# Layer 0 of a four-layer convolution stack: the patch filter and the 3x3 taps as one map of pixels per channel

## The chip, the cores and the metric

The kernel runs on one core of one Trainium2 chip. The metric is device time in microseconds (us). The median of three runs of the kernel before is 7,436.29 us (7,435.15 to 7,444.35).

## The reference, cut to what matters

The input x has the shape (4, 64, 256, 256) in 32-bit floats. Four layers follow one another, each `x = x + layer(groupnorm(x))`, with group normalization over pairs of channels. Only layer 0 is changed:

```python
x = einsum('bchw,oc->bohw', x, w_in)               # 64 -> 384 channels
xp = x in patches of 8 x 8 pixels
x  = irfft2(rfft2(xp) * fft_filter)                # one filter for each channel
x  = conv 3x3, each channel by itself (w_dw), padding 1
x1, x2 = split(x, 2)                               # 192 + 192 channels
x  = gelu(x1) * x2
x  = einsum('bchw,oc->bohw', x, w_out)             # 192 -> 64 channels
```

Both steps between the two einsums are linear in a channel's pixels. The patch filter is a circular convolution inside a patch. The 3x3 taps reach over the edge of a patch by one pixel. Layers 1 to 3 (a 3x3 convolution, a gated one with a threshold, a Fourier layer) are the same in both kernels.

## The kernel before, in words

Layer 0 is written in `_layer0`. An image has 256 rows; a step `t` of the main loop (line 659) takes 8 of them, one row of 32 patches, so that there are 4 x 32 steps and two more to finish. The order of the work on TensorE (PE), VectorE (DVE), ScalarE (ACT) and the queue of SyncE (SP) is written out by hand: inside `with ordered:` instructions run on each of these engines in the order of the program. GpSimd (POOL) is left to the scheduler; it clears borders and issues the stores.

Before the loop, statistics of the first image are gathered (line 312) from 32 loads of 512 KB. The statistics of later images are gathered inside the loop.

A step does the following:

- `normalize_x` (ACT, line 256) normalizes the input; pixels lie side by side on the partitions of two halves of the image.
- `transpose_x` and `transform_x` (PE, lines 396 and 406) turn the patches, so that pixels come to lie on partitions, and take the 64 x 64 patch DFT.
- `expand` (PE, line 419) multiplies by `w_in`, 64 to 384 channels, and DVE multiplies by the filter as it copies the result out of PSUM (line 422).
- `invert` (PE, line 457) takes the inverse DFT, and ACT copies the result into `y` (line 464), which holds 11 rows; the 3 last rows of the step before are copied from its `y` (line 437).
- `depthwise` (PE, line 484) does the nine taps of 256 of the 384 channels, as matmuls with diagonal 32 x 32 weights in sixteen array tiles, accumulated in PSUM. ACT takes the Gelu of the gate channels (line 498) and DVE multiplies by the value channels (line 504).
- `vector_tap` does the nine taps of the other 128 channels: the first on ACT (line 520), eight on DVE (line 522); Gelu and gate follow (lines 530 and 537).
- `project` (PE, lines 550 and 559) multiplies by `w_out`, DVE adds the residual (line 573) and takes the statistics for layer 1's normalization (line 581), and POOL issues the store (line 590).

All PSUM tiles of layer 0 come from `pair`, four tiles of two banks that are taken in turn. The gated result never leaves the core: it goes from `h` and `v` in SBUF into the last matmul.

Of the kernel before, what the change touches and what calls it, by code (L numbers as in the profile page):

```python
# [26 lines left out]
def _patch_dft():  # L27
# [20 lines left out]
    pick = np.array(pick)  # L48
    twice = lambda m: np.concatenate([m, m], 0)
    return twice(fwd.T), twice(inv.T), twice(pick).T  # L50
# [19 lines left out]
def _constants(H, W):  # L70
    f_blk, b_blk, pick = _patch_dft()
# [17 lines left out]
        "c_ident": np.eye(128), "c_avg32": avg32, "c_sel32": sel32, "c_fdft": f_blk, "c_bdft": b_blk, "c_pick": pick, "c_avg": avg, "c_avgp": avgp, "c_avgx": avgx,  # L89
# [5 lines left out]
def _layouts(i):  # L95


    order = np.r_[0:128, HID : HID + 128, 128:HID, HID + 128 : 2 * HID]
# [20 lines left out]
class _Net:  # L119
    def __init__(self, ctx, tc, a):  # L120
# [15 lines left out]
        self.slots = ctx.enter_context(tc.tile_pool(name="slot", bufs=2))  # L136
# [138 lines left out]
    def _layer0(self, ctx, dst):  # L275
# [9 lines left out]
        small = self.small = lambda name: pair(name)[:, 0, :]  # L285
        HW2 = W // 2
        NJ = H // 8
        NS = B * NJ
        Q = 32
        halves = [slice(0, C), slice(C, 128)]  # L290
        quarters = [slice(k * Q, (k + 1) * Q) for k in range(4)]

# [9 lines left out]
        with tc.tile_pool(name="l0a", bufs=1) as p_a:  # L302
            bst0 = new_bst0(0)

            flat = a["x"][0].rearrange("c (s h) w -> (c s) (h w)", s=2)
            avgs = [self.load(name, p_a) for name in ("c_avgp", "c_avgx")]
            for k in range(NJ):
                if k % 2 == 0:
                    two = self.slot(k // 2 % 3, f"st_{k}").rearrange("p r w -> p (r w)")
                t = two[:, 4 * W * (k % 2) : 4 * W * (k % 2 + 1)]  # L310
                nc.sync.dma_start(t, flat[:, 4 * W * k : 4 * W * (k + 1)])
                input_stats(t.rearrange("p (r w) -> p r w", w=W), k, bst0)
            self.group_norm(0, 0, bst0, avgs)

        cp = pool("l0c", 1)
        p_st, p_x, p_r, p_xn = pool("l0st", 2), pool("l0x", 2), pool("l0r", 2), pool("l0xn", 1)
        p_T, p_f, p_u, p_l = pool("l0xT", 1), pool("l0xf", 2), pool("l0up", 2), pool("l0l", 1)
        p_v, p_g, p_h = pool("l0v", 2), pool("l0g", 1), pool("l0h", 2)
        fdft, bdft = self.load("c_fdft", cp), self.load("c_bdft", cp)
        pick, filt = self.load("c_pick", cp), self.load("filt", cp)  # L320
        wdw = self.load("w_dw", cp)
        ps = small("psf")
        nc.tensor.matmul(ps[:, :384], pick, filt, start=True, stop=True)
        flt = cp.tile([128, 1, 384], F32, name="flt")
        nc.vector.tensor_copy(flt[:, 0, :], ps[:, :384])

        win = cp.tile([128, 384], F32, name="win")
        for s in range(2):
            nc.sync.dma_start(win[halves[s]], a["w_in"])

        wout = cp.tile([128, 4, C], F32, name="wout")
        for k in range(4):
            nc.sync.dma_start(wout[quarters[k]], a["w_out"][0:128].rearrange("(g q) o -> q g o", q=Q))
        woutc = cp.tile([128, C], F32, name="woutc")
        for s in range(2):
            nc.sync.dma_start(woutc[halves[s]], a["w_out"][128:HID])

        eye = cp.tile([128, Q], F32, name="eye")
        nc.vector.tensor_copy(eye, self.ident[:, 0:Q])
        for k in range(1, 4):  # L340
            nc.vector.tensor_add(eye, eye, self.ident[:, k * Q : (k + 1) * Q])
# [243 lines left out]
        def store(t, *sides, ins=None):  # L585
            if t not in rt:
                return
# [880 lines left out]
```

## Time and profile before

| what | value |
|---|---|
| median of the runs | 7,436.29 us |
| span of the profiled execution, first to last instruction | 7,394.8 us |
| its own time | taken as its span; the page gives no other |
| median over the span | 41.5 us |
| PE, PEld, DVE, ACT, POOL busy | 97%, 58%, 87%, 53%, 9% |
| mean granted PE clock | 0.971 |
| layer 0 in the span | 0 to 4,851.9 us |
| bytes moved by DMA in the whole span | 873.38 MB, mean 118 GB/s |

The page gives times in us, and means of one instruction in ns. A group's line has the line of the program, the engine, the operation, output<-input, shapes and count; then busy time and the mean of one; then the idle time before it and what ended it. For PE, a shape such as 64*32 is the array tile (rows x columns). A DMA share of 1 is all 16 DMA engines busy.

### The profile page before, as it was taken

Reading aid. Unit: us, or ns where it says so; the run is one execution under the profiler, and the core shown is the slowest. Engines: PE = TensorE matmul, PEld = TensorE weight load, DVE = VectorE, ACT = ScalarE, POOL = GpSimd, SP = SyncE. Lnnn points to the kernel's source line nnn. Section 1 sums busy time; section 2 is a strip of 40 time slices with the busy share of each in tenths; the row PEclk is TensorE's granted clock in tenths of the full one; section 3 lists DMA queues with packets and bytes.
Section 4 is the critical chain, followed back from the end, with each engine's and each line's share of the span. In section 5 each row is a group of like instructions: output and inputs, shape, how many; then the busy total and the mean of one; then the engine's idle time right before and its main releaser. Section 6 shows DMA issues by size and latency. Waiting matters only on the chain. (4 is left out here: it accounts for less than half of the span.)

```text
span 7394.8 us, 396673 instructions
## 1 busy us (share of the span) xinstructions
PE 7148.3 (97%) x188280; PEld 4274.7 (58%) x188280; DVE 6436.5 (87%) x5625; ACT 3928.6 (53%) x4181; POOL 659.3 (9%) x1435
## 2 busy tenths in 40 slices
PE   6999999999999999999999999999999999999998
PEld 4666666666666666666666666633334444444376
DVE  7999999999999999999999999889988888897445
ACT  3444444454454444444445545457778778776211
POOL 0000000000000000000000000011111222222011
PEclk9999999999999999999999999999999999999955
DMA  3222222222222222222111111279986676676989
GB/s 131 64 64 64 61 64 61 61 61 61 61 61 61 61 61 61 61 61 61 47 46 47 47 47 47 60 186 228 230 197 158 169 178 173 172 179 192 354 328 400
DMA packets 650136, 873.38 MB, mean 118 GB/s; under 512 B 43988, under 2 KB 470180, under 8 KB 646468
## 3 DMA queue, kind: packets, MB, share of 16 engines
q1 hardware_dynamic: 567492, 579.51, 29.4%
q0 software_dynamic: 81024, 268.50, 12.5%
q8 instruction: 1477, 24.20, 1.4%
q14 instruction: 143, 1.17, 0.1%
HBM read 579.41 MB, written 268.44 MB: 115 GB/s over the span
## 5 line engine op out<-in xcount | busy, mean ns | idle before, releaser
L484 PE MATMUL psd<-y,diag 32*32 32x512 f32 x73296 | 2535.6, 597 | 12.4 <-issue 10.7
L522 DVE SCALAR_TENSOR_TENSOR v<-y,sb_w_dw,v 128x2048 f32<-128x2048 f32 x1024 | 2391.5, 2335 | 112.1 <-ACT v L520 89.3
L484 PEld LDWEIGHTS psd<-y,diag 32*32 32x32 f32 x73296 | 1526.9, 103 | 858.8 <-issue 338.9
L464 ACT COPY y<-psy 128x512 f32<-128x512 f32 x1536 | 915.6, 660 | 1673.5 <-PE psy L457 1671.7
L422 DVE TENSOR_TENSOR up<-psu,flt 128x768 f32<-128x768 f32 x1024 | 933.1, 952 | 203.9 <-PE psu L419 203.2
L457 PEld LDWEIGHTS psy<-sb_c_bdft,up 64*64 64x64 f32 x49152 | 850.2, 135 | 343.3 <-issue 129.8
L457 PE MATMUL psy<-sb_c_bdft,up 64*64 64x64 f32 x49152 | 919.5, 221 | 25.0 <-issue 22.4
L419 PE MATMUL psu<-win,xf 64*64 64x384 f32 x8192 | 785.0, 488 | 20.9 <-DVE h L504 10.4
L1040 DVE TENSOR_TENSOR q<-xn 128x2313 f32<-128x2313 f32 (+2 forms) x256 | 627.8, 2494 | 1.7 <-ACT xn L256 1.7
L1095 PE MATMUL one<-z,wp 32*32 32x512 f32 x16384 | 594.1, 598 | 17.3 <-issue 13.4
L1041 ACT ACTIVATE q<-q 128x2313 f32<-128x2313 f32 (+2 forms) x256 | 528.9, 2086 | 31.4 <-DVE q L1040 29.9
L498 ACT ACTIVATE h<-psd 128x1024 f32<-128x1024 f32 x258 | 251.2, 1023 | 519.8 <-PE psd L484 519.7
L256 ACT ACTIVATE xn<-x,nb,r 128x1024 f32<-128x1024 f32 (+3 forms) x272 | 486.9, 1793 | 22.2 <-DMA x<-x 8.3
L1095 PEld LDWEIGHTS one<-z,wp 32*32 32x32 f32 x16384 | 368.4, 103 | 225.0 <-issue 82.7
L1054 PE MATMUL div<-q,ones 64*32 64x512 f32 x8192 | 466.2, 594 | 14.3 <-ACT q L1041 9.4
L429 POOL MEMSET y<- 128x22 f32 x384 | 52.2, 136 | 4264.3 <-ACT y L437 3209.8
L419 PEld LDWEIGHTS psu<-win,xf 64*64 64x64 f32 x8192 | 299.5, 134 | 192.1 <-issue 87.7
L1128 POOL DMA_DIRECT2D x<-r x512 | 273.6, 541 | 972.1 <-DVE r L1125 881.2
L854 PE MATMUL m<-t,wk 64*64 64x512 f32 x3072 | 341.1, 588 | 0.0
L1054 PEld LDWEIGHTS div<-q,ones 64*32 64x32 f32 x8192 | 151.8, 107 | 321.1 <-issue 253.6
L537 DVE TENSOR_TENSOR v<-g,v 64x1024 f32<-64x1024 f32 x257 | 313.2, 1219 | 9.3 <-ACT g L530 1.4
L504 DVE TENSOR_TENSOR h<-h,psd 128x1024 f32<-128x1024 f32 x258 | 302.7, 1215 | 7.5 <-PE psd L484 7.0
(156 smaller groups left out, 7400.4 us busy)
## 6 DMA issues: line engine op xcount, KB each, us to landing
x<-x SPq DMA_DIRECT2D x240, 640.0 KB, 6.3
x<-x SPq DMA_DIRECT2D x100, 1024.0 KB, 13.9
x<-in_x_dram SPq DMA_DIRECT2D x256, 256.0 KB, 3.8
x<-o POOLq DMA_DIRECT2D x128, 512.0 KB, 8.1
r<-x SPq DMA_DIRECT2D x512, 128.0 KB, 4.0
x<-r POOLq DMA_DIRECT2D x512, 128.0 KB, 4.0
r<-in_x_dram SPq DMA_DIRECT2D x248, 256.0 KB, 3.8
x<-r POOLq DMA_DIRECT2D x248, 256.0 KB, 3.3
```

The lines of the kernel that those rows point to most:

```text
L256: self.nc.scalar.activation(dst, src, AF.Identity, bias=self.nb[n][p0:p1, b : b + 1], scale=self.r[n][p0:p1, b : b + 1])
L419: nc.tensor.matmul(ps[halves[n], s, 0:384], xf[t][halves[s], n, 4 * g + k], win[halves[s]], start=True, stop=True)
L422: nc.vector.tensor_mul(ups[t, g][:, :, k, :], ps[:, :, 0:384], flt.broadcast_to([128, 2, 384]))
L457: nc.tensor.matmul(ps[halves[c], n, s, :, k, :], up[halves[n], s, k, i * 128 + c * C : i * 128 + (c + 1) * C], bdft[halves[n]], start=True ...
L464: nc.scalar.copy(yt[t][i][:, 3:11, w0 : w0 + 64].rearrange("p r (k n w) -> p n r k w", k=4, n=2), ps[:, :, s])
L484: ins = nc.tensor.matmul(d[q // 2][quarters[j], q % 2], diag[quarters[q], i, k, :], rows_in(t, i, quarters[q], j, dy)[:, :, dx : dx + W], ...
L522: nc.vector.scalar_tensor_tensor(v, s, wdw[:, 2, k : k + 1], v, ALU.mult, ALU.add)
L854: nc.tensor.matmul(rows2(m)[halves[j], s], w[dx][halves[s]], ts[n][halves[s], i, 2 * j : 2 * j + 2, dx : dx + W], start=(dx == 0), stop=(d ...
L1040: nc.vector.tensor_sub(d, p0, p1)
L1041: nc.scalar.activation(d, d, AF.Square)
L1054: ins = nc.tensor.matmul(ps[quarters[j], h], ones[halves[h]], q[n, g, k][halves[h], r + 2 * j : r + 2 * j + 2, o : o + W], start=(m == 0), ...
L1095: ins = nc.tensor.matmul(rows2(ps[g])[quarters[j], k], w[quarters[i]], z[quarters[i], h, 2 * j + dy : 2 * j + dy + 2, dx : dx + W], tile_p ...
```

## The change

Layer 0 is written anew; layers 1 to 3 stay. The patch filter and the taps of a channel become one linear map from the pixels of a patch and its neighbours to output pixels. `tables` works the map's coefficients out on the chip, from `fft_filter`, `w_dw` and a constant. `weights` spreads them into tiles `T` and writes them to a DRAM scratch `wts`, 2 x 64 x 64 x 112 numbers for each of three groups of 128 channels (64 gates and their 64 values). Two tiles `T`, one after the other, share one buffer.

The main loop runs over 20 blocks `p`, five for each image, of 7, 7, 7, 6 and 6 rows of patches. For each group of channels `kb`:

- `expand` makes the 128 channels for up to 8 rows of patches. The patch's 64 normalized pixels are the stationary operand, `w_in` the moving one, so that the result has pixels on partitions with no transpose and no DFT. ACT and DVE copy it out by turns into `u`, one tile with patches as columns (33 for each row of patches, the first of them zero).
- `load_w` brings map tiles from DRAM, one for two calls of `convolve`, through four buffers, requested three tiles ahead.
- `convolve` takes four gates and their four values, in eight array tiles of 64 x 32, with up to 231 patches as columns. One matmul makes the 32 output pixels that need only their own patch; four, accumulated, make the other 32, from the patch, its right, its lower and its diagonal neighbour. ACT takes the Gelu, DVE the gate, and POOL stores the result `h` (four buffers) into a DRAM scratch `g`.

While block `p` is worked on, block `p - 1` is finished in eight units, one for each row of pixels within a patch. `load_g` reads the gated result back with channels on partitions and loads the residual; `project` multiplies by `w_out`, adds the residual, takes the statistics and stores. Units follow the expansion of each group and its maps 5 and 10. SP issues `load_w`, `load_g`, the input and the statistics' loads in the order of the program. The `slots` pool, which layer 0 shared with layer 1, is made after layer 0.

```diff
-    order = np.r_[0:128, HID : HID + 128, 128:HID, HID + 128 : 2 * HID]
+    order = np.concatenate([np.r_[k : k + C, HID + k : HID + k + C] for k in range(0, HID, C)])
...
-        def transform_x(t):
...
-                        nc.tensor.matmul(
-                            ps[halves[s], n, k], x[halves[n], k, halves[s]], fdft[halves[n]], start=True, stop=True
-                        )
...
-        def expand(t, g, k):
...
-                    nc.tensor.matmul(
-                        ps[halves[n], s, 0:384], xf[t][halves[s], n, 4 * g + k], win[halves[s]], start=True, stop=True
-                    )
-            nc.vector.tensor_mul(ups[t, g][:, :, k, :], ps[:, :, 0:384], flt.broadcast_to([128, 2, 384]))
...
-                            nc.tensor.matmul(
-                                ps[halves[c], n, s, :, k, :],
-                                up[halves[n], s, k, i * 128 + c * C : i * 128 + (c + 1) * C],
-                                bdft[halves[n]], start=True, stop=True,
-                            )
...
-                        ins = nc.tensor.matmul(
-                            d[q // 2][quarters[j], q % 2], diag[quarters[q], i, k, :],
-                            rows_in(t, i, quarters[q], j, dy)[:, :, dx : dx + W],
-                            start=(k == 0), stop=(k == 8), tile_position=(q * Q, j * Q),
-                        )
...
-                    nc.vector.scalar_tensor_tensor(v, s, wdw[:, 2, k : k + 1], v, ALU.mult, ALU.add)
...
+        blocks = []
+        for b in range(B):
+            i0, sizes = -1, [7, 7, 7, 6, 6]
+            for n in sizes:
+                blocks.append((b, i0, n))
+                i0 += n
+        NB = len(blocks)
+        u = pool("l0u", 1).tile([128, C, 8 * CW + 2], F32, name="u")
+        p_xn, p_x, p_st = pool("l0xn", 8), pool("l0x", 2), pool("l0st", 2)
+        p_w, p_h = pool("l0w", 4), pool("l0h", 4)
...
+        wts = [dr.tile([2, 64, C, NC], F32, name=f"wt{t}") for t in range(KB)]
...
+        def tables(t):
+            ps = self.small(f"kx_{t}")
+            nc.tensor.matmul(ps[:, 0:289], filt[:, 128 * t : 128 * (t + 1)], kext, start=True, stop=True)
+            nc.vector.tensor_copy(kx.rearrange("p u v -> p (u v)"), ps[:, 0:289])
...
+        def weights(t, copies):
+            for hh in range(2):
+                T = p_a.tile([128, 4, 8, NC], F32, tag="T", name=f"T_{t}_{hh}")
...
+                    copies[k % len(copies)](d, s)
+                for h in range(2):
+                    (nc.sync if t == 0 else nc.gpsimd).dma_start(
+                        wts[t][h, 32 * hh : 32 * hh + 32].rearrange("i c n -> c i n"),
+                        T[halves[h]].rearrange("p a b n -> p (a b) n"),
+                    )
...
+        def expand(p, kb, t, mc):
+            b, i0, n = blocks[p]
+            ps = pair(f"psu_{p}_{kb}_{t}_{mc}")
+            xn = xns[b, i0 + t]
+            for m in range(8):
+                for s in range(2):
+                    for h in range(2):
+                        nc.tensor.matmul(
+                            ps[halves[h], s, m * C : (m + 1) * C],
+                            xn[halves[s], 8 * mc + m].rearrange("p r w -> p (r w)"),
+                            win[halves[s], kb * 128 + h * C : kb * 128 + (h + 1) * C], start=True, stop=True,
+                        )
+            d = u[:, :, t * CW + 1 : (t + 1) * CW].rearrange("p c (s h m) -> p h s c m", s=2, h=2)[:, mc]
+            v = ps.rearrange("p s (m c) -> p s c m", m=8)
+            if mc == 0:
+                nc.scalar.copy(d, v)
+            else:
+                nc.vector.tensor_copy(d, v)
+        def load_w(p, j):
+            if p >= NB:
+                return
+            w = wl[p, j] = p_w.tile([128, 8, NC], F32, tag="w", name=f"w_{p}_{j}")
+            nc.sync.dma_start(
+                w, wts[j // 8][:, :, 8 * (j % 8) : 8 * (j % 8) + 8].rearrange("h i c n -> (h i) c n")
+            )
+        UNITS = ((32, 32, 0), (64, 16, 1), (80, 28, CW), (108, 4, CW + 1))
+        def convolve(p, kb, g):
+            L = CW * blocks[p][2]
+            ps = pair(f"pc_{p}_{kb}_{g}")
+            w = wl[p, 8 * kb + g // 2]
+            tile_of = lambda q, h: dict(tile_position=(h * C, q * Q))
+            for q in range(4):
+                for h in range(2):
+                    nc.tensor.matmul(
+                        ps[quarters[q], h, 0:L], w[halves[h], 4 * (g % 2) + q, 0:32], u[halves[h], 4 * g + q, 0:L],
+                        start=True, stop=True, **tile_of(q, h),
+                    )
+            for k, (c0, m, o) in enumerate(UNITS):
+                for q in range(4):
+                    for h in range(2):
+                        nc.tensor.matmul(
+                            ps[q * Q : q * Q + m, h, L : 2 * L], w[halves[h], 4 * (g % 2) + q, c0 : c0 + m],
+                            u[halves[h], 4 * g + q, o : o + L], start=(k == 0), stop=(k == 3), **tile_of(q, h),
+                        )
+            h = p_h.tile([128, 2 * 7 * CW], F32, tag="h", name=f"h_{p}_{kb}_{g}")[:, 0 : 2 * L]
+            nc.scalar.activation(h, ps[:, 0, 0 : 2 * L], AF.Gelu)
+            nc.vector.tensor_mul(h, h, ps[:, 1, 0 : 2 * L])
+            if p not in gs:
+                gs[p] = p_g.tile([2, HID, Q, L], F32, tag=f"g{L}", name=f"g_{p}")
+            c = kb * C + 4 * g
+            nc.gpsimd.dma_start(
+                gs[p][:, c : c + 4].rearrange("a c p l -> (c p) a l"), h.rearrange("p (a l) -> p a l", a=2)
+            )
...
+        def load_g(p, r):
...
+            g1 = p_1.tile([128, P * 7 * CW], F32, tag="g1", name=f"g1_{p}_{r}")[:, 0 : P * L]
+            g6 = p_6.tile([128, 4 * 7 * CW], F32, tag="g6", name=f"g6_{p}_{r}")[:, 0 : 4 * L]
...
+            for s, p0, q0, m in planes(r):
+                nc.sync.dma_start(g1[:, q0 : q0 + m], gs[p][s, 0:128, p0 : p0 + m])
+                for k in range(2):
+                    lo, hi = max(q0, 4 * k), min(q0 + m, 4 * k + 4)
+                    if lo < hi:
+                        nc.sync.dma_start(
+                            g6[halves[k], lo - 4 * k : hi - 4 * k], gs[p][s, 128:HID, p0 + lo - q0 : p0 + hi - q0]
+                        )
+            rt = rts[p, r] = p_r.tile([128, 7, HW2], F32, tag="r", name=f"r_{p}_{r}")[:, 0 : hi - lo]
+            for s in range(2):
+                nc.sync.dma_start(
+                    rt[halves[s]], xr(a["x"][b], b)[rr][:, j0 : j0 + hi - lo, s * HW2 : (s + 1) * HW2]
+                )
...
+            po = pair(f"po_{p}_{r}")
...
+            for k, q0, q1, d, c0, c1 in groups:
+                for s in range(2):
+                    nc.tensor.matmul(
+                        result(k, q0, q1, c0, c1, s), wo1, moving(g1, q0, q1, d, s),
+                        start=(c0 == 0), stop=False, skip_group_check=True,
+                    )
...
+                    nc.tensor.matmul(
+                        result(k, q0, q1, c0, c1, s), wo6[halves[k]],
+                        moving(g6[halves[k]], q0 - 4 * k, q1 - 4 * k, d, s),
+                        start=False, stop=True, tile_position=(k * C, s * C), skip_group_check=True,
+                    )
...
+                nc.vector.tensor_add(
+                    v, v, po[:, k, c0:c1].rearrange("p (i q j) -> p i q j", i=m, q=q1 - q0)
+                )
...
+            for s in range(2):
+                nc.gpsimd.dma_start(xr(dst[b], b)[rr][:, j0 : j0 + m, s * HW2 : (s + 1) * HW2], rt[halves[s]])
...
+            weights(0, [nc.scalar.copy, nc.vector.tensor_copy, nc.gpsimd.tensor_copy])
...
+            for j in range(3):
+                load_w(0, j)
...
+            for p in range(NB + 1):
+                if p == 1:
+                    ctx_a.close()
+                    p_1, p_6, p_r = pool("l0g1", 2), pool("l0g6", 2), pool("l0r", 3)
+                    load_g(0, 0)
+                    load_g(0, 1)
+                def unit():
+                    r = next(units, None)
+                    if r is None:
+                        return
+                    project(p - 1, r)
+                    k = 8 * (p - 1) + r + 2
+                    if k < 8 * p:
+                        load_g(*divmod(k, 8))
...
+                for kb in range(KB):
+                    for t in range(n + 1):
+                        if 0 <= i0 + t < NP:
+                            for mc in range(2):
+                                expand(p, kb, t, mc)
...
+                    unit()
+                    for g in range(16):
+                        j = 8 * kb + g // 2 + 3
+                        if g % 2 == 0:
+                            load_w(p + j // 24, j % 24)
+                        convolve(p, kb, g)
+                        self.next_norms()
+                        if p == 0 and kb < 2 and g == 0:
+                            tables(kb + 1)
+                            weights(kb + 1, [nc.gpsimd.tensor_copy])
...
+                        if g in (5, 10):
+                            unit()
...
+                for r in units:
+                    project(p - 1, r)
+                if p >= 1:
+                    load_g(p, 0)
+                    load_g(p, 1)
```

## The prediction

> **What bounds the kernel now.** I read the page from the top. The change touches layer 0 alone, so the first question is how much of the span layer 0 is and what limits it.
>
> ```profile
> span 7394.8 us, 396673 instructions
> PE 7148.3 (97%) x188280; PEld 4274.7 (58%) x188280; DVE 6436.5 (87%) x5625; ACT 3928.6 (53%) x4181; POOL 659.3 (9%) x1435
> L484 PE MATMUL psd<-y,diag 32*32 32x512 f32 x73296 | 2535.6, 597 | 12.4 <-issue 10.7
> L522 DVE SCALAR_TENSOR_TENSOR v<-y,sb_w_dw,v 128x2048 f32<-128x2048 f32 x1024 | 2391.5, 2335 | 112.1 <-ACT v L520 89.3
> L457 PE MATMUL psy<-sb_c_bdft,up 64*64 64x64 f32 x49152 | 919.5, 221 | 25.0 <-issue 22.4
> L1054 PE MATMUL div<-q,ones 64*32 64x512 f32 x8192 | 466.2, 594 | 14.3 <-ACT q L1041 9.4
> ```
>
> To see: PE is the bound, and two thirds of its time are layer 0's taps (L484), inverse DFT (L457) and expansion (L419), work that the change replaces. The third line prices a 32x32 tile, the last a 64x32 tile, the shape that the change uses.
>
> Then windows. Layer 0 runs from 0 to 4851.9, where the chain of waits has its first long piece, L854 of layer 1.
>
> ```profile
> 0.00:90.00 90.00, 27.22 (x636) 18.75 (x636) 57.66 (x106) 14.21 (x19) 4.67 (x20) 1.00 0.61 216
> 90.00:4850.00 4760.00, 4688.68 (x150099) 3091.26 (x150096) 4382.56 (x3601) 2330.40 (x2939) 245.66 (x679) 1.00 0.24 58
> 4850.00:5550.00 700.00, 679.39 (x6324) 244.27 (x6324) 614.63 (x588) 499.31 (x403) 80.11 (x144) 0.99 0.88 214
> 7240.00:7300.00 60.00, 51.74 (x256) 41.55 (x250) 30.78 (x50) 7.51 (x13) 9.37 (x13) 0.50 1.04 414
> ```
>
> Columns: stretch, length, busy PE, PEld, DVE, ACT, POOL, clock, DMA share, GB/s. To see: in 90-4850 PE is busy 98.5%, DVE 92%, DMA only 24%. GB/s divided by share is what the DMA engines give when full: 242 in layer 0 (mostly 512-byte runs), 243 in layer 1 (1 KB rows landing at a pitch of 1,032 bytes), 398 at the end (runs of 2 KB and more). No window passes a share of 1.04.
>
> [...] the end window with both queues is full at 1.04. [...] in layer 1 about a fifth of the 1 KB packets took some 46 ns, the rest 64 to 115. [...] L484's psd is evicted in 1.02 us (ACT) and 1.22 us (DVE) per 1,024 elements. [...] the last window shows 0.50 while its DMA is full.
>
> **The change, part by part.** It removes all PE work of layer 0 (4,689 us busy), L522 (2,391), L422 (933) and the copies L437, L464.
>
> PE, added. Maps: 20 blocks x 3 x 16 x 40 = 38,400 matmuls in eight tiles, mean 33 x 6.6 = 218 columns. L1054 gives 466.2/8192 x 8 = 455 ns per eight of 512 columns, 0.89 ns a column: 4,800 x 218 x 0.89 = 930 us. L484's 16 tiles took 553 ns for 512 columns, 98 more; if that is an exposed weight load it adds 4,800 x 98 ns = 470. Expansion: 144 patch rows x 3 x 64 = 27,648 matmuls of 64 columns at L457's 18.7 ns: 517. Last conv: 160 units of some 845 + 422 column times: 180. PE 1,630 to 2,100.
>
> DVE. L504 (1,024 elements, 1,215 ns) and the 512-element L573 (682) give 149 ns + 1.04 per element from PSUM. Gates 960 x 603 ns = 579; half of the evictions, 432 x 1.21 = 525; residual adds 160 x 1.33 = 212 (a stride of 8 elements may double it: the strided L1301 took 600 ns for 256); statistics of the output 189, of the next batch 175. Sum 1,680. ACT: 432 x 1.02 + 960 x 0.53 + 128 normalizations x 1.24 = 1,110.
>
> Order: `u` has one buffer, so each of the 60 expand stages starts when the last map before it is done, and the first map waits for all 16 evictions: some 10 us of eviction, then some 20 of maps, gates and projection. About 30 x 60 x 0.95 = 1,700 to 2,000 us if nothing else held it.
>
> DMA, added. (a) The map tiles come again for each block: 480 x 459 KB = 220 MB in 3,584-byte runs, at 398: 555 us. (b) The gated result is written, 214 MB in 960 x 256 runs of 924 or 792 bytes at any address. Nearest: layer 0's 512-byte store runs; a 4 KB packet of eight took 338 ns in the trace, against 160 to 180 for whole ones, so 194 GB/s. Bounds: 398 (538 us) and a doubling of my value. I take 180: 1,190 us, 77 ns a run. (c) It is read back, 214 MB in runs of 0.8 to 5.5 KB, mostly unaligned in SBUF: between 398 and 243, I take 310: 690. (d) Input, residual, statistics and output are the same bytes as before and nearly the same runs: 0.24 x 4,760 = 1,142, less some 100 of instruction fetch for twice as many instructions: 1,000. (e) Tables: 11 MB in 448-byte runs: 45. Sum 3,480 us of all 16 engines, twice the compute path. So the bound moves from PE to DMA. The cover of 24% share that hid every transfer is gone.
>
> Waits. SP issues in one order[...]: a map load stands behind the reads of g and the residual, which wait for a unit's buffers and, at a block's end, for all stores of g. It is requested three tiles ahead. POOL issues 960 stores beside 320 of the output, at some 0.7 us (L590: 686 ns): 900 us, hidden. `h` has four buffers, so a slow store holds the Gelu four maps later. Full engines make both late together, which is the DMA bound again.
>
> Ends. Start: before, 90 us to the first tap; the first table adds copies and two writes from one buffer, and in block 0 POOL builds two more tables ahead of its stores: I take 180. End: eight units of the last block with nothing beside them, and layer 1's loads no longer ahead of its buffers: 85.
>
> Sum: 3,480 at a share of 0.98 is 3,550, + 265 = 3,815 for layer 0, in place of 4,852. The profiled execution's own time is its span 7,394.8; the rest after layer 0 stays 2,543. Span after 6,358; the median stands 41.5 over the span: 6,400 us. Differences under 0.2% are about what a measurement here can't tell from no change.
>
> **Rivals.** (1) The DMA works near its best: unaligned runs cost as little as whole ones. (b) and (c) fall to 538 each, sum 2,680, at share 1.04 2,580 + 265: layer 0 2,845, time 5,430. [...] Against: the 64 to 115 ns packets of layer 1. Compute alone would be lower still, but cannot go under this floor. I give 5,400 to 6,000 a chance of 0.22.
>
> (2) My forecast, 6,000 to 6,800: 0.50.
>
> (3) DMA and compute take turns. In expansion only three map tiles and a few stores can be in the air; with PE waiting, its clock falls to 0.5 as in layer 3, expansion becomes 16 us of PE and the maps 2.1 us each. Then some 8 us per stage run with idle DMA engines: + 60 x 8 = 480 us, 6,880; with dearer reads of g up to 7,400. For: the end windows have exactly this clock. Against: stores in flight and prefetch cover part. 0.19.
>
> (4) Slower than before, by one mechanism: the 245,760 unaligned store runs. [...] it decides from the point where layer 0 reaches 4,867: (4,867 - 265) x 0.98 = 4,510 of DMA, so 2,220 for (b), 145 ns a run against my 77. At 170 ns: 2,610, time 7,850. For: no row shows an unaligned store to DRAM. Against: even unaligned 1 KB loads stay under 115 ns. 0.08; the last 0.01 is for no change.
>
> **Numbers.** Range: 5,500 to 7,200 leaves out the best of (1), the end of (3) and (4), less than 2 in 10. The likeliest case's own range is 6,000 to 6,800. Faster 0.91, same 0.01, slower 0.08.
>
> **What the profile after would show.** The DMA share near 0.95 to 1.0 and 250 to 300 GB/s all through layer 0; PE under 60% busy, clock below 1; waits on map tiles from DMA and of Gelu on stores; 8-tile groups of maps of some 200 ns at full clock; store packets of g at some 300 ns for four runs. If share stays under 0.8 the turn-taking of (3) holds; if PE or DVE is over 90% busy, my DMA prices are too high. I would be wrong by most if unaligned runs cost much less or more than 77 ns, or if strided evictions double and make DVE the bound.

## The result, and the profile after

The changed kernel takes 8,017.83 us (median of four runs, 8,005.01 to 8,033.69), the kernel before beside it 7,438.93 (four runs, 7,435.15 to 7,444.35): a ratio of 1.0776, with a 95% interval of 1.0759 to 1.0794. The prediction was 6,400 us. The change makes the kernel slower by 580 us, on the side to which the prediction gave 0.08.

The page of the changed kernel, the lines that answer to those shown of before; `div` at L1020 is the old L1054.

```profile
span 8002.3 us, 369156 instructions
PE 6107.3 (76%) x173528; PEld 3999.4 (50%) x173528; DVE 3770.1 (47%) x4504; ACT 2725.7 (34%) x2772; POOL 1411.1 (18%) x2198
...
PE 72%; issue 20%; DMA 5%; DVE 2%; ACT 1%; POOL 1%; SPq 0%; DVEq 0%; POOLq 0%; ACTq 0%
...
L476 PE MATMUL pc<-u,w 64*16 64x231 f32 (+7 forms) x61440 | 2036.8, 373 | 661.4 <-issue 660.4
L438 PE MATMUL psu<-win,xn 64*64 64x64 f32 x55296 | 1053.7, 238 | 685.9 <-issue 666.3
L469 PE MATMUL pc<-u,w 64*32 64x231 f32 (+1 forms) x15360 | 788.4, 370 | 245.1 <-issue 191.2
L1020 PE MATMUL div<-q,ones 64*32 64x512 f32 x8192 | 467.4, 598 | 11.2 <-ACT q L1007 9.4
```

To see: PE has done less than before in all (6,107 us against 7,148), VectorE 2,666 us less, and yet the span is 607.5 us longer. The line of the chain is the new thing. In the chain of work that ended last a fifth of the span is "issue": PE waited for nothing that the profile shows. The idle times of the two maps (L476, L469) and of the expansion (L438) are 1,592 us together, 1,518 of them issue. Layer 0 ends at 5,452 us in place of 4,852; the rest takes 2,550 in place of 2,543.

The windows that answer to those of before: the start, layer 0, a piece of layer 1, the end.

```profile
0.00:138.00 138.00, 7.01 (x196) 6.04 (x200) 58.90 (x112) 8.36 (x25) 14.84 (x30) 1.00 0.64 177
138.00:5400.00 5262.00, 3641.76 (x135652) 2822.00 (x135643) 1696.00 (x2435) 1126.65 (x1519) 976.11 (x1416) 0.90 0.61 173
5460.00:6160.00 700.00, 680.08 (x6368) 241.31 (x6368) 614.04 (x586) 505.08 (x405) 81.47 (x145) 0.99 0.90 220
7850.00:7910.00 60.00, 50.11 (x247) 40.52 (x244) 28.93 (x47) 7.27 (x12) 9.05 (x12) 0.50 1.04 412
```

To see: in layer 0 no engine is full. PE is busy for 69%, the DMA engines for 61% and not for the forecast 95 to 100%, VectorE for 32%. So the bound is none of the resources that the prediction weighed. What the idle PE waits for is seen in the order of its instructions, here in the expansion (start, duration, name, and in brackets the idle time before it):

```profile
2500.25 2.09 PE L438 MATMUL psu<-win,xn 64*64 64x64 f32 x128 [1.65 <-issue]
2504.27 2.09 PE L438 MATMUL psu<-win,xn 64*64 64x64 f32 x128 [1.93 <-issue]
2508.01 2.09 PE L438 MATMUL psu<-win,xn 64*64 64x64 f32 x128 [1.65 <-issue]
2511.49 1.15 PE L438 MATMUL psu<-win,xn 64*64 64x64 f32 x62 [1.38 <-issue]
```

PE runs exactly 128 matmuls without a break and then stands for 1.4 to 1.9 us, again and again. Nothing in the program has this period: a tile of the expansion ends after 64 records. With its weight load each matmul is two instructions, so a run is 256 instructions. The page's DMA queues show what has this size:

```profile
q8 instruction: 1360, 22.28, 1.2%
```

And of the kernel before:

```profile
q8 instruction: 1477, 24.20, 1.4%
```

22.28 MB in 1,360 packets are 16,382 bytes a packet; over 256 instructions that is 64 bytes each. The number fits too: PE's 2 x 173,528 instructions are 1,356 blocks of 256, and before, 2 x 188,280 are 1,471. PE stops at the end of a block of its own instruction stream. Between 200 and 5,400 us it is idle for 1,593 us, and 1,577 of those are in 775 pauses over 0.4 us. Of these, 539 come 127 or 128 matmuls after the one before, and most others after twice or three times as many.

The times of the packets tie the two together. Of the 757 pauses over 0.4 us that end in "issue", 734 end 1.2 to 1.7 us after a packet of q8 has landed; a time taken at random lies in that band in one case of ten. Between two such pauses that are 127 or 128 matmuls apart (534 cases) there is always exactly one packet, and it starts at the earliest 1.04 us after PE has resumed. So in these stretches the packet of the next block started only once the block before it had begun to run.

This gives the theory tested below, **S**: TensorE is starved of instructions. A block of 256 was fetched every 3.3 to 3.4 us at best (the first percentile of the time from one fetch to the next, in the kernel before, after, and with less traffic alike; medians 3.92 us before and 4.33 after). In the expansion this time is made of 1.1 us from PE's resuming to the start of the packet, 1.1 us for the packet, and 1.4 us from its landing to PE's next resuming (medians). A block of the expansion holds only 2.09 us of work, one of the maps mostly 2.9 to 3.5. In the kernel before a block of taps holds 128 x 553/16 ns = 4.4 us, enough to hide the fetch: the taps idled for 12.4 us in all. The rival **C** is that the array's own time sets the pace: columns streamed and weights loaded. A second question is whether the fetch, which is itself a DMA, is delayed by the transfers of data.

### The profile page after: what moved, and what is told of

The parts are those of the page before. It is cut to its first block, busy times and chain, and to the rows that moved or that the text cites. A ratio compares the mean times of both kernels' runs of the same rounds, so it can differ in the third digit from the quotient of the medians.

```text
span 8002.3 us, 369156 instructions
## 1 busy us (share of the span) xinstructions
PE 6107.3 (76%) x173528; PEld 3999.4 (50%) x173528; DVE 3770.1 (47%) x4504; ACT 2725.7 (34%) x2772; POOL 1411.1 (18%) x2198
## 3 DMA queue, kind: packets, MB, share of 16 engines
q8 instruction: 1360, 22.28, 1.2%
## 4 chain that ended last, share of the span: by engine, by line
PE 72%; issue 20%; DMA 5%; DVE 2%; ACT 1%; POOL 1%; SPq 0%; DVEq 0%; POOLq 0%; ACTq 0%
PE pc L476 21%; PE psu L438 13%; PE m L820 8%; PE one L1061 7%; PE div L1020 5%; PE pc L469 5%; PE po L553 3%; PE po L559 2%; PE psz L1050 2%; PE psa L1248 2%; PE psy L1395 1%; DMA x<-x 1%; PE zero L1061 1%; DMA st<-in_x_dram 1%; DMA b<-x 1%
## 5 line engine op out<-in xcount | busy, mean ns | idle before, releaser
L476 PE MATMUL pc<-u,w 64*16 64x231 f32 (+7 forms) x61440 | 2036.8, 373 | 661.4 <-issue 660.4
L476 PEld LDWEIGHTS pc<-u,w 64*16 64x16 f32 (+3 forms) x61440 | 1389.9, 102 | 1034.1 <-issue 841.4
L438 PE MATMUL psu<-win,xn 64*64 64x64 f32 x55296 | 1053.7, 238 | 685.9 <-issue 666.3
L481 ACT ACTIVATE h<-pc 128x462 f32<-128x462 f32 (+1 forms) x960 | 513.5, 535 | 2946.2 <-PE pc L476 2827.3
L482 DVE TENSOR_TENSOR h<-h,pc 128x462 f32<-128x462 f32 (+1 forms) x960 | 581.0, 606 | 1924.8 <-ACT h L481 1922.5
L438 PEld LDWEIGHTS psu<-win,xn 64*64 64x64 f32 x55296 | 985.1, 152 | 773.6 <-issue 750.7
L448 DVE COPY u<-psu 128x1024 f32<-128x1024 f32 x432 | 529.4, 1225 | 1196.1 <-PE psu L438 1196.1
L486 POOL DMA_DIRECT2D g<-h x960 | 691.6, 721 | 2186.8 <-DVE h L482 2062.1
L469 PE MATMUL pc<-u,w 64*32 64x231 f32 (+1 forms) x15360 | 788.4, 370 | 245.1 <-issue 191.2
L446 ACT COPY u<-psu 128x1024 f32<-128x1024 f32 x432 | 469.5, 1087 | 1159.1 <-PE psu L438 1159.1
L469 PEld LDWEIGHTS pc<-u,w 64*32 64x32 f32 x15360 | 397.6, 112 | 355.8 <-issue 255.1
L1020 PE MATMUL div<-q,ones 64*32 64x512 f32 x8192 | 467.4, 598 | 11.2 <-ACT q L1007 9.4
```

The costliest lines, as they stand in the source:

```text
L438: nc.tensor.matmul(ps[halves[h], s, m * C : (m + 1) * C], xn[halves[s], 8 * mc + m].rearrange("p r w -> p (r w)"), win[halves[s], kb * 128 ...
L448: nc.vector.tensor_copy(d, v)
L469: nc.tensor.matmul(ps[quarters[q], h, 0:L], w[halves[h], 4 * (g % 2) + q, 0:32], u[halves[h], 4 * g + q, 0:L], start=True, stop=True, **ti ...
L476: nc.tensor.matmul(ps[q * Q : q * Q + m, h, L : 2 * L], w[halves[h], 4 * (g % 2) + q, c0 : c0 + m], u[halves[h], 4 * g + q, o : o + L], st ...
L482: nc.vector.tensor_mul(h, h, ps[:, 1, 0 : 2 * L])
L486: nc.gpsimd.dma_start(gs[p][:, c : c + 4].rearrange("a c p l -> (c p) a l"), h.rearrange("p (a l) -> p a l", a=2))
```

## The experiments

Each run is held against runs of the kernel before on the same chip: 7,385.78 us for the first group (few columns, less traffic, the first wide expansion), 7,389.60 for the second (fewer matmuls, longer matmuls, six copies, the second wide expansion), 7,396.09 for the third (two copies, the third wide expansion), 7,398.29 for the last experiment. Runs of the first two groups were timed once. The changed kernel, run again with the third group, took 7,986.10 there, 1.0804 times the kernel before (1.0772 to 1.0835); 7,980 to 7,985 is therefore its place beside the first two groups.

**Fewer columns, the same instructions.** Three of the five maps stream 32 columns in place of up to 231.

```diff
-    ps[q * Q : q * Q + m, h, L : 2 * L], ...
-    u[halves[h], 4 * g + q, o : o + L], ...
+    ps[q * Q : q * Q + m, h, L : L + (L if k == 0 else 32)], ...
+    u[halves[h], 4 * g + q, o : o + (L if k == 0 else 32)], ...
```

> Three of the five matmuls of each map (the right, lower and diagonal neighbours) stream 32 columns in place of 231 or 198, so their sums are incomplete; every instruction, transfer and wait stays. Theory S (TensorE waits for its own instruction stream at every 128th matmul): time within 4% of the 8,018 us, 7,700 to 8,050, because the blocks that get shorter wait longer. Rival C (the column work of the doubled matmul records sets the pace): 46,080 of 76,800 map records lose 85% of their columns, some 0.5 of 1,860 us of column time at clock 0.9, so 6,950 to 7,150.

Measured: 7,883.44 us, some 97 less than the changed kernel. The group of the maps, from the page:

```profile
L476 PE MATMUL pc<-u,w 64*4 64x32 f32 (+4 forms) x61440 | 1266.2, 260 | 901.0 <-issue 900.6
```

To see: 771 us of busy time are gone from the maps at L476, and 240 us of them come back as more idle time before the same instructions. The two maps' lines overlap; counted once, their busy time fell by 552 us (from 2,180). The rest comes back in L469's pauses and in a longer expansion and last matmul, at a mean clock in layer 0 that fell from 0.90 to 0.81. The time lies in S's range: the columns hardly mattered, and C falls as the main cause.

**Fewer instructions, about the same columns as that.** The three neighbour maps are left out.

```diff
-            for k, (c0, m, o) in enumerate(UNITS):
+            for k, (c0, m, o) in enumerate(UNITS[:1]):
-                            ..., start=(k == 0), stop=(k == 3), **tile_of(q, h),
+                            ..., start=True, stop=True, **tile_of(q, h),
```

> The matmuls of the right, lower and diagonal neighbours are left out (their terms are missing from the sums): 46,080 of 134,000 matmul records of layer 0, or 360 of 1,050 blocks of 128, with their 46,080 weight loads; transfers as in the changed kernel. The run with few columns left out nearly the same column work and kept the instructions, and took 7,883. Theory S: 360 blocks less at 3.7 to 5.7 us each, 1,300 to 2,000 us faster than 8,018: 6,000 to 6,700. Rival B (data transfers pace the layer; 3,200 us of all engines stay): not below 7,300.

Measured: 7,154.84 us, some 830 less than the changed kernel and 730 less than with few columns. The direction is S's, but the time lies in neither expected range. Two groups of the page show why, and after them the window 500 to 4,000:

```profile
L481 ACT ACTIVATE h<-pc 128x462 f32<-128x462 f32 (+1 forms) x960 | 508.1, 533 | 2143.0 <-DMA g<-h 1462.1
L469 PE MATMUL pc<-u,w 64*32 64x231 f32 (+1 forms) x15360 | 732.8, 431 | 858.8 <-DMA w<-wt 415.3
```

```profile
500.00:4000.00 3500.00, 2090.62 (x71462) 1520.81 (x71457) 1322.94 (x1958) 889.60 (x1214) 745.49 (x1036) 0.81 0.75 210
```

Once PE's stream is shorter, the Gelu waits for stores of `g` that hold its four buffers, and the maps wait for their tiles. The waits for DMA that the prediction expected exist, but they come only behind the stream, at about 7,150 us.

**A longer matmul in the expansion, the same instructions.** Seven of every eight matmuls stream 112 columns in place of 64; the next one overwrites what is too much.

```diff
-    ps[halves[h], s, m * C : (m + 1) * C],
+    ps[halves[h], s, m * C : m * C + (112 if m < 7 else C)],
-    win[halves[s], kb * 128 + h * C : kb * 128 + (h + 1) * C], ...
+    win[halves[s], kb * 128 + h * C : kb * 128 + h * C + (112 if m < 7 else C)], ...
```

> The changed kernel, but seven of eight matmuls of the expansion stream 112 columns in place of 64; the 48 extra results are overwritten by the next matmul. Column work of the expansion x1.66, its instructions the same. Theory S: a block of 128 then has 3.4 us of columns, still within a fetch: less than 150 us slower, 7,950 to 8,150. Rival C: + 0.66 x 1,034 = 680 us, 8,600 to 8,750.

Measured: 8,003.28 us, 1.083 times the kernel before, where the changed kernel stands at 1.0804.

```profile
L438 PE MATMUL psu<-win,xn 64*64 64x112 f32 (+1 forms) x55296 | 1446.7, 262 | 332.9 <-issue 319.6
```

To see: PE's busy time in the expansion rose by 393 us (from 1,053.7) and its pauses fell by 353 (from 685.9). Added work fills the pauses and costs some 20 us in all, where C asked for 680: S holds, C falls for the expansion too.

**Less traffic.** First the three map tiles of the first group's beginning are kept in SBUF and used for all (the other tiles are never read, 220 MB less); then, with that, `g` is neither stored nor read and the last matmul takes zeros (648 MB less in all).

```diff
+            if (p, j) > (0, 2):
+                wl[p, j] = wl[0, j % 3]
+                return
```

> The first three map tiles stay in SBUF and serve all channels (the maps of other channels are wrong); 477 loads of 448 KB, 220 MB, and SP's waits for their buffers are gone. TensorE's instructions are the same. Rival B (TensorE waits for transfers of data): 500 to 900 us faster. Theory S alone, with a fixed time for an instruction fetch: less than 100 us faster. Theory S with fetches that stand behind data in the DMA engines: stalls of 1,560 us shrink by a fifth to a third, 300 to 500 us faster.

```diff
-            nc.gpsimd.dma_start(gs[p][:, c : c + 4]..., h...)
-            g1 = p_1.tile(...)
-            g6 = p_6.tile(...)
+            if not flat_g:
+                flat_g.append(cp.tile([128, P * 7 * CW], F32, name="flat_g"))
+                nc.gpsimd.memset(flat_g[0], 0.0)
+            g1, g6 = flat_g[0][:, 0 : P * L], flat_g[0][:, 0 : 4 * L]
...
-                nc.sync.dma_start(g1..., gs[p]...)
-                        nc.sync.dma_start(g6..., gs[p]...)
```

> As the run with kept maps, and the gated result is neither stored nor read back (a tile of zeros goes into the last conv, so the layer's output is its residual alone): 648 MB less in all. TensorE's instructions are the same. Theory S with a fixed fetch: some 128 matmuls per 3.5 us or more still, 7,300 to 7,800. Theory S with fetches behind data: stalls fall by more than half, layer 0 near 4,200 to 4,500, 6,750 to 7,100. Rival B: the same direction, but then the stalls would not stay at every 128th matmul.

Measured: 7,599.59 and 6,991.74 us, some 380 and 990 less than the changed kernel. Two groups of the second, and after them its window of layer 0:

```profile
L480 PE MATMUL pc<-u,w 64*32 64x231 f32 (+7 forms) x61440 | 1855.2, 351 | 259.2 <-issue 256.5
L439 PE MATMUL psu<-win,xn 64*64 64x64 f32 x55296 | 944.2, 223 | 627.9 <-issue 611.5
```

```profile
138.00:4400.00 4262.00, 3289.58 (x135266) 2624.36 (x135266) 1684.06 (x2414) 1121.14 (x1513) 274.98 (x452) 0.98 0.29 63
```

To see: two different parts. The maps' pauses fall from 661 to 259 us: that part was a fetch made late by data. The expansion's stay at 628: its 2.09 us of work a block are under the 3.3 us of the quickest fetches, and it pauses at a DMA share of 0.29 as it did at 0.61. The time from fetch to fetch tells the same (median 3.78 us, 95% below 5.37; in the changed kernel 4.33 and 7.38), while the fetch's own packet takes about 1.1 us in every kernel, so the delay lies ahead of the packet. Between pauses one block apart, the median from PE's resuming to the start of the packet is 3.75 us in the maps of the changed kernel and 1.59 us here; in the expansion it is 1.14 us in both. What holds the packet back, other transfers on its DMA engines or the memory behind them, no run here shows. With shorter pauses the clock rises from 0.90 to 0.98. The trace of the changed kernel has the two side by side: in layer 0 its clock is 1.00 or 0.50; in the 3.4 us before each of the 218 stretches at 0.50 (1,007 us together) PE was busy for at most 58%, and before each return to 1.00 for at least 76%. In this run the long pauses still come at block ends, but for some 2% of their time.

**Traffic added to the kernel before.** If data delay the fetch, then transfers that nobody waits for must slow down the old kernel. Copies of 1 MB from DRAM to DRAM, six for each step of the main loop, then two. Here are the six; the two are issued at `k == 3` alone.

```diff
                     f(*args, ins=ins)
+                if k in (3, 6):
+                    traffic(6 * t + 3 * i + k // 3, ins)
...
+        def traffic(k, ins=None):
+            d = nc.gpsimd.dma_start(heap[k % 8], flat_x[256 * (k % 64) : 256 * (k % 64) + 256])
...
-                    gate_part(t, depthwise(t, 0, *loads))
+                    gate_part(t, depthwise(t, 0, *loads, (traffic, 6 * t)))
...
-                    d = depthwise(t, 1, *moves)
+                    d = depthwise(t, 1, *moves, (traffic, 6 * t + 3))
```

> The kernel before, with six copies of 1 MB from the input to an unused DRAM scratch in each step of layer 0, issued by POOL and paced by TensorE; nothing reads them. DMA share of layer 0 near 0.6, as in the changed kernel. Theory S with fetches behind data: stalls at every 128th matmul appear, where the kernel before has none, and layer 0 grows by 300 to 1,200 us: 7,700 to 8,600. A fixed fetch time, or no part of instruction fetches: under 100 us slower, 7,390 to 7,500.

> The kernel before with two unused 1 MB copies a step in place of six (six took 8,733 against 7,390, at a DMA share of 0.57). DMA share near 0.35. Theory S: a block's work of 4.0 to 4.2 us covers a fetch of 3.4 us and some delay, so most is still hidden: 50 to 450 us slower than before. A rival for the six copies, that they slow the kernel through POOL's queue or through other data's lateness and not through fetches: in proportion, 400 to 500 us slower, with waits on POOL, ACT or DMA and not on the instruction stream.

Measured: 8,733.17 us (+1,344, 133 beyond the expected range) with six, 7,842.93 us with two (+447; ratio 1.061, 1.0579 to 1.0641). The taps of the first, from the page, and after them its window 500 to 4,000:

```profile
L484 PE MATMUL psd<-y,diag 32*32 32x512 f32 x73296 | 2840.2, 652 | 470.4 <-issue 466.1
```

```profile
500.00:4000.00 3500.00, 2986.15 (x86836) 1863.44 (x86808) 2552.05 (x2113) 1346.72 (x1699) 363.84 (x838) 0.92 0.57 181
```

And the same two views of the second:

```profile
L484 PE MATMUL psd<-y,diag 32*32 32x512 f32 x73296 | 2650.5, 614 | 148.9 <-issue 144.8
```

```profile
500.00:4000.00 3500.00, 3277.06 (x101280) 2128.30 (x101268) 2970.53 (x2461) 1572.01 (x1983) 259.39 (x634) 0.98 0.38 107
```

The same window of the kernel before:

```profile
500.00:4000.00 3500.00, 3460.11 (x111107) 2285.43 (x111079) 3249.51 (x2686) 1721.88 (x2175) 183.69 (x509) 1.00 0.24 59
```

To see: the taps read nothing that the copies touch, and their idle time grows from 12.4 us to 149 and 470, nearly all of it issue. In that window PE was idle for 40 us before, for 223 with two copies and for 514 with six. The +447 us with two copies lies in the range of S and in that of its rival alike, so the waits have to decide. Over layer 0, PE's pauses above 0.15 us that end in issue are 35 us before, 309 with two copies and 859 with six; its pauses for any other engine or a DMA are 96, 97 and 116 together. The rest of the added time is PE's own: its busy time in the whole span rose from 7,148 us to 7,318 and 7,640, at a clock in the window of 1.00, 0.98 and 0.92. The DMA share of 0.57 is far from full. So a share of 0.38 already cost this kernel time; its PE had little to spare from one block of instructions to the next (4.4 us of taps a block, a median of 3.92 us from fetch to fetch without the copies).

**Half as many instructions in the expansion.** 128 columns of `w_in` stream past 64 stationary pixels, so 13,824 matmuls do what 27,648 did; the result lies in PSUM otherwise and is copied in four pieces. Three ways to share these between ACT and DVE:

```diff
-            for m in range(8):
+            for m in range(4):
                 for s in range(2):
-                    for h in range(2):
+                    for c in range(2):
                         nc.tensor.matmul(
-                            ps[halves[h], s, m * C : (m + 1) * C],
-                            xn[halves[s], 8 * mc + m]...,
-                            win[halves[s], kb * 128 + h * C : kb * 128 + (h + 1) * C], ...
+                            ps[halves[c], s, m * 128 : (m + 1) * 128],
+                            xn[halves[s], 8 * c + 4 * mc + m]...,
+                            win[halves[s], kb * 128 : (kb + 1) * 128], ...
...
+            for c in range(2):
+                for h in range(2):
+                    copy = nc.scalar.copy if c == h else nc.vector.tensor_copy
+                    copy(d[halves[h], c, mc], v[halves[c], h])
```

That is the first; the second decides by `h == 0`, the third by `mc == 0`, so that one PSUM tile is one engine's.

> Expansion with 128 columns for each stationary patch in place of 64 for gates and 64 for values: half its matmuls, the same columns; outputs of patches 8 to 15 of a half land on the other partitions, and the copies out of PSUM shift them (four of 64 partitions in place of one of 128). Theory S: expansion's blocks of 128 matmuls hold 3.8 us of columns, as long as a fetch, so its 666 us of stalls mostly go, while copies cost up to 200 more: 7,350 to 7,650. Rival C (column work): no gain, 8,000 to 8,250 for the dearer copies.

> The wide expansion again, with ACT copying the gates and DVE the values, so that they write different partitions of u and do not wait for each other (1,330 and 1,279 us of such waits in the first form). Copies then take some 1.4 us per engine and PSUM tile, 8 rows x 2 x 1.4 = 22 us for a stage in place of the 28 to 30 that expansion took with its fetch stalls. Theory S: 200 to 450 us faster than the changed kernel, 7,550 to 7,800. Rival C (column work): no gain.

> The wide expansion a third time: ACT copies the whole of one PSUM tile, DVE the whole of the next, as in the changed kernel, so that neither waits for the other within a tile. A stage's copies take 8 x 4 x 0.68 = 22 us, its 128-column matmuls 16 us, against some 30 us for expansion in the changed kernel. Theory S: 200 to 500 us faster than the changed kernel, 7,500 to 7,800; most of the issue waits of expansion gone. Rival C (column work alone): no faster than the changed kernel.

Measured: 8,616.34, 8,086.18 and 7,529.69 us (the last timed: 1.0186 times the kernel before, 1.0147 to 1.0225). The first two miss their expected ranges by far and say nothing on S, since the copies hold them. Here the copies of the first:

```profile
L448 DVE COPY u<-psu 64x512 f32<-64x512 f32 x1728 | 1214.1, 703 | 1291.1 <-ACT u L448 1279.3
L448 ACT COPY u<-psu 64x512 f32<-64x512 f32 x1728 | 1136.7, 658 | 1433.4 <-DVE u L448 1331.7
```

The two engines wait for one another by turns, though they write different parts of `u`, and in the second they still do (764 and 712 us). The third has ACT take one PSUM tile and DVE the next. They still share `u`, but no PSUM tile, and these waits are gone:

```profile
q8 instruction: 1147, 18.79, 1.1%
...
L448 DVE COPY u<-psu 64x512 f32<-64x512 f32 x1728 | 1215.1, 703 | 187.7 <-PE psu L438 157.9
L476 PE MATMUL pc<-u,w 64*32 64x231 f32 (+7 forms) x61440 | 2063.5, 373 | 653.1 <-issue 652.6
L438 PE MATMUL psu<-win,xn 64*64 64x128 f32 x27648 | 944.5, 284 | 289.9 <-DVE u L448 122.8
```

To see: 213 blocks fewer are fetched and 456 us saved against the changed kernel beside it (7,986.10), 2.1 us a block. The expansion's pauses fall from 686 to 290 us and are now mostly waits for copies (87 us are issue); the maps' stay as they were. The columns are as many as before, so C, which asked for no gain, falls again.

> The changed kernel itself, for times on this chip beside those of the runs below. Every theory: 1.07 to 1.08 of the kernel before, 7,940 to 8,030.

The repeat is the 7,986.10 us used above.

**Fewer instructions in the maps.** On top of the third, the two maps that read the patch's own pixels become one of 64 output pixels. The sums of the neighbours are accumulated into one half of a larger tile's output; the output is not the map's, and the run is read for its time alone.

```diff
-                        ps[quarters[q], h, 0:L], w[halves[h], 4 * (g % 2) + q, 0:32], u[halves[h], 4 * g + q, 0:L],
-                        start=True, stop=True, **tile_of(q, h),
+                        ps[halves[q % 2], h, d], w[halves[h], 4 * (g % 2) + q, 0:64], u[halves[h], 4 * g + q, 0:L],
+                        start=True, stop=False, **tile_of(q, h, 0),
...
-            for k, (c0, m, o) in enumerate(UNITS):
+            for k, (c0, m, o) in enumerate(UNITS[1:]):
...
-                            ps[q * Q : q * Q + m, h, L : 2 * L], ...
+                            ps[p0 : p0 + m, h, d], ...
```

> The expansion as in e9_wide_expand_by_tile, and the two maps of a channel that read the patch's own pixels made into one of 64 output pixels: a call of the maps issues 32 matmuls (64 records) in place of 40 (80), while their columns cost more, since 64x64 tiles run four at a time and the three neighbour maps now use only four of the eight tiles: eight turns of some 206 ns (0.89 ns x 231) in place of five, 1,490 us in place of 930. S (TensorE is starved of instructions): 15,360 fewer records are 120 blocks fewer, at some 4.3 us a block up to 516 us; the added columns lie within the time of the fetch (1.65 us of work a call against half a block, 2.15 us). Against e9 (7,530): 7,030 to 7,250, faster than the kernel before. The queue of instructions falls from 1,147 packets to about 1,027. C (the array's time sets the maps): 560 us more columns, 7,800 to 8,100.

Measured: 7,544.03 us, 1.0202 times the kernel before (1.0184 to 1.022), against 1.0186 without this edit: nothing gained. S's range was missed by 294 us, and C's lay 256 us above the time. The two groups of the maps, and after them the window of layer 0:

```profile
L479 PE MATMUL pc<-u,w 64*16 64x231 f32 (+5 forms) x46080 | 2321.4, 345 | 5.0 <-issue 4.8
L470 PE MATMUL pc<-u,w 64*64 64x231 f32 (+1 forms) x15360 | 986.6, 357 | 98.8 <-DVE u L448 67.5
```

```profile
138.00:4900.00 4762.00, 4428.80 (x92418) 2723.22 (x92422) 2374.18 (x3704) 1794.37 (x2810) 967.97 (x1408) 0.99 0.66 189
```

To see: the pauses for instructions are gone (653 us to 5), at a DMA share of 0.66 and with the maps otherwise fed as before. PE is busy for 93% of the window at a clock of 0.99, so here C is the bound: a call of the maps takes 2.97 us at 198 columns, two of them, one block, 5.9 us, well above the usual fetch (a median of 4.33 us in the changed kernel). Four records of 64x64 tiles make a turn, as the kernel before shows: one of 512 columns took 111 ns there (L854, 341.1 us for 3,072), four 444 ns, and eight of 64x32 tiles 455 (L1054). My expectation reckoned eight turns of the array a call; but the price of a turn is per record, and there are two records to a matmul: sixteen turns of 0.89 x 198 = 176 ns are 2.82 us. The same slip had been made in the prediction, as the next section shows. It also shows the limit of S: here the work lasted longer than the fetch and hid it, and then it was the work that counted.

No kernel here that does the whole computation is faster than the kernel before. A way to fewer instructions without more array time (twice the patches a map, for one) was not built.

## Why the prediction was wrong, by its own steps

- **"PE, added"** is the first step that failed, by a factor of two. By itself it would not have missed the sign. It took 38,400 and 27,648 matmuls from the program and prices per record from the profile. But a matmul of these kernels leaves two records, each with a weight load: L476 and L469 have 76,800, L438 55,296. The kernel before had it in plain sight: its 8,192 records of L1054 and 49,152 of L457 are 4,096 and 24,576 matmuls in the program. Twice the low sum, 2 x (930 + 517 + 180) = 3,254, is about what PE did: 3,290 us without traffic, 3,642 in the changed kernel at a clock of 0.90. The same slip stands in "twice as many instructions" for the kernel before: the windows of layer 0 hold 150,099 matmul records before and 135,652 after, so the stream of instructions hardly became shorter. Counted rightly, PE alone would have stood near the DMA's 3,480, and the largest gains would have been off the table.
- **"So the bound moves from PE to DMA"** is the step that missed the sign. The sum held no term for the time that PE waits for its own instructions; the fetch stood in it only as "some 100 of instruction fetch" among the bytes. What fills layer 0's 5,262 us is 3,642 us of PE and some 1,600 of pauses, nearly all of them issue at the ends of blocks. An estimate from these figures: PE's 3,290 us at nearly full clock with the two ends, 138 and 74, would be some 3,500 for layer 0, against 4,852 before, so the pauses and the clock that fell with them are what turned the sign. "The cover of 24% share that hid every transfer is gone" was right in a way not meant: among the transfers so hidden was the fetch.
- **DMA sum**: 3,480 forecast, 0.61 x 5,262 = 3,210 measured, so 8% off; but this is luck in part, since its terms were off in both directions. (b), the stores of `g`, took 626 us of all 16 engines in that window and not 1,190: most go out as packets of 4,620 bytes, five runs of 924, with a median of 194 ns, 39 ns a run against "77 ns a run". The evidence of unaligned loads in layer 1 did not carry over to stores. (a), the map loads, took 717 us against 555: the median packet of 3,584 bytes took the 140 ns that were reckoned with, the mean 188. (c), the reads of `g`, took 748 against 690, and all the rest 1,117 against 1,045.
- **DVE 1,680 and ACT 1,110**: right, 1,696 and 1,127 us in the window. The strided operands that "may double it" did not decide anything: DVE was 32% busy. PE's "two thirds" for L484, L457 and L419 was a slip without weight: the three are 59% of its time, layer 0 as a whole 66%.
- **Order, "1,700 to 2,000 us if nothing else held it"**: wrong with the count of PE's work on which it rested.
- **Start 180 and end 85**: about right. The first expansion starts at 133.9 us, the first map at 171.5; layer 0 closes 74 us after its last map, some 60 of them units that wait for `g` from DMA.
- **"The median stands 41.5 over the span"**: not so in general. The profiled execution of after is itself one of the runs, 8,005.01 us at a span of 8,002.3; the rest is what executions differ by.
- **Rival 3, turn-taking.** Its sign, "if share stays under 0.8", came, and the clock fell to 0.90; but its cause is not the one that the runs show, and a low share alone doesn't tell the two apart. The period of 128 matmuls does.
- **Rival 4** got the sign right and the mechanism wrong: 145 ns a store run would have been needed, and a median of 39 was measured.

## What to carry to other kernels

Count PE's work in records of the profile, not in matmuls of the program. Then ask of each stretch of several blocks how much time 128 of its matmuls take: below the time of one fetch (here 3.3 us at best, a median of 4.33 with data moving) PE paused at the end of each block, the profile called it "issue", and fewer instructions or less traffic helped, while longer ones filled the pauses (353 us fewer in the expansion). A short run did no harm: the inverse DFT of the kernel before has 2.4 us of work in 128 records, but came in runs of 64 between longer work, and idled for 25 us in all. The kernel before, which stood just above the line with 4.4 us a block of taps, paid for transfers long before the DMA engines were full: 447 us at a share of 0.38.

## What had not been expected of the hardware

Fetches of instructions were delayed by data at a DMA share of 0.38 already: +447 us for two copies of 1 MB a step, +1,344 for six. Between them the cost rose about in proportion to the bytes (3.0 times for three times as many). Lengthening the expansion's matmuls from 64 to 112 columns cost some 20 us of 8,003, against 393 us of added PE time. And pauses cost twice here: with them the granted clock was 0.90 over layer 0, 0.81 with few columns, and 0.98 to 0.99 where they were short or gone, so that PE's own work took longer too (3,642 us in place of 3,290 for the same matmuls).
